# Four graph-attention layers over sixteen graphs: one-head weights by halves of the targets, a new timetable for the preparation of steps

## The chip, the cores and the metric

The kernel runs on one core of one Trainium2 chip. The metric is the device time of one execution in microseconds (us); the engines of the core are TensorE (PE, with its weight loads PEld), VectorE (DVE), ScalarE (ACT), GpSimd (POOL) and SyncE (SP, which here only issues transfers).

## The reference

x is 16 graphs x 1024 nodes x 256 features, adj one 1024 x 1024 matrix for all of them. Four layers follow each other; layers 0 and 2 have 4 heads of 64 features, layers 1 and 3 one head of 256:

```
h = relu(layernorm(x))
q = h @ W_l                                     # N x 256, as H heads of D
e[i, j] = leaky_relu(q_i . a_src + q_j . a_dst) # masked by adj[i, j]
x = x + act(softmax_j(e) @ q)                   # act: elu, in the last layer relu
```

All of it is float32. In the kernel exp(e[i, j]) is, up to factors of i alone, exp(slope * e_dst[j]) * max(G[i], R[j]), with G a row over the targets i and R a column over the sources j. So a block of softmax weights is one VectorE instruction, `max(G, R[j]) * mask`, and the sum of a softmax row is one more column of q.

## The kernel before

A **step** is one layer of one graph (64 steps, 32 with four heads and 32 with one). Four graphs are under way at a time, and `order_of_steps` lets them take turns; the order is mostly 4-head, 1-head, 4-head, 1-head, but in every eight steps two 4-head steps (13 and 14, 21 and 22, ..., 53 and 54) and two 1-head steps (17 and 18, ...) are neighbours. Steps 0, 1, 2 have four heads.

**Aggregation** of a step is cut into 8 groups (L323-326). A group of a 4-head step is one head and half of the targets: 64 matmuls (128 records in the profile, since a float32 matmul shows as two). A group of a 1-head step is 128 targets: 8 matmuls, 16 records. A group reads tiles `w` (L249): one tile holds the weights of 128 sources to all 1024 targets, a head has 8 of them, and a group of either kind needs all 8 sources' tiles. There are 19 buffers of `w`. The sums `acc` go to `y` on ACT (L270).

**Weights** (L250) are written by DVE, one tile an instruction, out of the head's row G. That row is made in the step's preparation: TensorE transposes it (L223), it goes to DRAM as `grow` (L227), comes back broadcast over the partitions as `gs` (L239, SP queue), and ACT copies it to PSUM as `g` (L245).

**Preparation** of a step (L149-234) is 18 pieces: statistics in two halves (DVE, L161-162, then four small POOL instructions, L165-169), normalisation (ACT, L175), transposes (PE, L183, then ACT, L184), eight projections (PE, L195, each followed by three ACT instructions, with four heads by one of POOL too), `factors` (ACT) and `rows` (L222-227).

**Finish** of a step (L274-318): the reciprocal on DVE (L287), the scaling on POOL, the exponential on ACT (L300), the maximum on DVE (L306), the sum into x on POOL (L307); after the last layer the store, and then the load of the next graph, on SP.

**Order.** Under `tc.manual_schedule()` (L387) every engine executes in the order in which the program emits. Time in the emission is counted in groups: 8 * step + group. The preparation of step n + 2 is planned at the start of step n, or at its group 4 if the graph's previous layer was step n - 1; `PREPARATION` gives the distance of each piece, `rows` at 9. As soon as `rows` of a step is emitted, its G may be fetched and copied, and DVE's tiles follow: 4 a group in a 4-head step, 2 in a 1-head step, as far as buffers allow. What follows a group in the emission: pieces of the finish of the step before, pieces of the preparation, tiles. The preparations of steps 0 and 1 stand ahead of the manual region, where the framework orders the instructions.

The lines that matter for the order:

```
            for k, (h, i0, per) in enumerate(groups(n)):
                if n + 2 < len(steps) and k == (0 if ready_at[n + 2] < n - 1 else 4):
                    plan(n + 2, 8 * n + k)
                emit_tiles(place[n, h, C - 1] + 1, must=True)
                aggregate(n, h, i0, per)
```

Of the kernel before, what the change touches and what calls it, by code (L numbers as in the profile page):

```python
# [24 lines left out]
F32 = mybir.dt.float32  # L25
# [4 lines left out]
ALU = mybir.AluOpType  # L30
# [3 lines left out]
P = 128  # L34
# [1 line left out]
SHIFT = 60.0  # L36
EXP_SHIFT = math.exp(SHIFT)
STREAMS = 4
WBUFS = 19
PREPARATION = (0, 0, 1, 2, 3, 3, 4, 4, 5, 5, 5, 5, 6, 6, 7, 7, 8, 9)  # L40


LAYERS = [
# [8 lines left out]
def kernel(ctx: ExitStack, tc: tile.TileContext, x, adj, ws, avs, out):  # L52
    nc = tc.nc
    B, N, F = x.shape
    C = N // P
    K = F // P
    HALF = C // 2
# [70 lines left out]
            for m, op in ((0, ALU.is_gt), (1, ALU.not_equal)):  # L128
                nc.vector.tensor_scalar(masks[m][:, :, ic * P:(ic + 1) * P], pm, 0.0, None, op0=op)

    xpool = ctx.enter_context(tc.tile_pool(name="xpool", bufs=STREAMS))
    prep = ctx.enter_context(tc.tile_pool(name="prep", bufs=2))
    small = ctx.enter_context(tc.tile_pool(name="small", bufs=4))
    work = ctx.enter_context(tc.tile_pool(name="work", bufs=2))
# [7 lines left out]
    xs = {}  # L142
    state = [dict() for _ in steps]

    def load(b):
        xs[b] = xpool.tile([P, C, F], F32, name="x")
        nc.sync.dma_start(out=xs[b], in_=x[b].rearrange("(c p) f -> p c f", p=P))

    def preparation(n):  # L149
# [19 lines left out]
                nc.gpsimd.tensor_scalar(shift, shift, -1.0, None, op0=ALU.mult)  # L169

        def normalise(half):
            xn = st["xn", half] = prep.tile([P, HALF, F], F32, name="t4", bufs=3)
            for q in range(HALF):
                c = half * HALF + q
                nc.scalar.activation(xn[:, q, :], xs[b][:, c, :], AF.Identity,  # L175
                                     bias=st["shift"][:, c:c + 1], scale=st["rstd"][:, c:c + 1])
# [54 lines left out]
            out += [lambda half=half, k=k: transpose(half, k) for k in range(K)]  # L231
            out += [lambda c=c: project(c) for c in range(half * HALF, (half + 1) * HALF)]

        return list(zip(PREPARATION, out + [factors, rows], strict=True))

    def fetch(n, h):

        gs = state[n]["gs", h] = work.tile([P, N], F32, name="gs", bufs=2)
        nc.sync.dma_start(out=gs, in_=state[n]["grow"][h].rearrange("c i -> (c i)")  # L239
                          .partition_broadcast(P))  # L240

# [2 lines left out]
        g = state[n]["g", h] = ps_g.tile([P, N], F32, name="g")  # L244
        nc.scalar.activation(g, state[n]["gs", h], AF.Copy)  # L245

    def weights(n, h, jc):

        w = state[n]["w", h, jc] = work.tile([P, N], F32, name="w", bufs=WBUFS)  # L249
        nc.vector.scalar_tensor_tensor(w, state[n]["g", h], state[n]["rcol"][:, jc, h:h + 1],  # L250
                                       masks[LAYERS[steps[n][1]][3]][:, jc, :],
                                       op0=ALU.max, op1=ALU.mult)

    def aggregate(n, h, i0, per):
        H = LAYERS[steps[n][1]][0]
        D = F // H
        st = state[n]
        if h == 0 and i0 == 0:
            st["y"] = work.tile([P, C, H, D + 1], F32, name="y")
        acc = ps_acc.tile([P, per, D + 1], F32, name="acc")  # L260
        cols = P // 2 if H > 1 else P
        for q in range(per):
            for jc in range(C):

                for o in range((i0 + q) * P, (i0 + q + 1) * P, cols):
                    nc.tensor.matmul(acc[o % P:o % P + cols, q, :],  # L266
                                     lhsT=st["w", h, jc][:, o:o + cols],
                                     rhs=st["whx"][:, jc, h, :], start=(jc == 0),
                                     stop=(jc == C - 1))
        nc.scalar.activation(st["y"][:, i0:i0 + per, h, :], acc, AF.Copy)  # L270

    def finish(n):

        b, l = steps[n]  # L274
        H = LAYERS[l][0]
        D = F // H
        st = state[n]

        def views(half):
            s = slice(half * HALF, (half + 1) * HALF)  # L280
            return (xs[b][:, s, :].rearrange("p c (h d) -> p (c h) d", h=H),
                    st["y"][:, s, :, 0:D].rearrange("p c h d -> p (c h) d"),
                    st["r"][:, s, :].rearrange("p c h -> p (c h)"))

        def divide():
            st["r"] = small.tile([P, C, H], F32, name="r")
            nc.vector.reciprocal(st["r"], st["y"][:, :, :, D])  # L287

        def scaled(half):
            xh, yh, r = views(half)  # L290
            nc.gpsimd.tensor_tensor(yh, yh, r[:, :, None].to_broadcast([P, HALF * H, D]),  # L291
                                    op=ALU.mult)
            if l < L - 1:

                e = st["e", half] = prep.tile([P, HALF * H, D], F32, name="t4", bufs=3)
                nc.gpsimd.tensor_scalar(e, yh, 0.0, -3.0e38, op0=ALU.min, op1=ALU.max)  # L296

        def exponential(half):
            if l < L - 1:
                nc.scalar.activation(st["e", half], st["e", half], AF.Exp)  # L300

        def add(half):
            xh, yh, r = views(half)
            if l < L - 1:
                e = st["e", half]
                nc.vector.scalar_tensor_tensor(e, e, -1.0, yh, op0=ALU.add, op1=ALU.max)  # L306
                nc.gpsimd.tensor_add(xh, xh, e)  # L307
                return
            nc.vector.scalar_tensor_tensor(xh, yh, 0.0, xh, op0=ALU.max, op1=ALU.add)
            nc.sync.dma_start(  # L310
                out=out[b, half * HALF * P:(half + 1) * HALF * P, :].rearrange(
                    "(c p) f -> p c f", p=P), in_=xs[b][:, half * HALF:(half + 1) * HALF, :])
            if half == 1 and b + STREAMS < B:
                load(b + STREAMS)

        return [(0, divide), (0, lambda: scaled(0)), (1, lambda: scaled(1)),
                (1, lambda: exponential(0)), (2, lambda: exponential(1)),
                (2, lambda: add(0)), (3, lambda: add(1))]

    def groups(n):  # L323
        if LAYERS[steps[n][1]][0] == 1:
            return [(0, i, 1) for i in range(C)]
        return [(h, i, HALF) for h in range(LAYERS[steps[n][1]][0]) for i in (0, HALF)]

    tiles = [(n, h, jc) for n, (b, l) in enumerate(steps) for h in range(LAYERS[l][0])
             for jc in range(C)]
    place = {t: i for i, t in enumerate(tiles)}  # L330
    done = {"tiles": 0, "g": 0, "gs": 0, "free": 0, "prepared": 0, "wanted": 0}
    agenda = []

    def prepare(upto):

        while agenda and (agenda[0][0] <= upto or agenda[0][1] < done["wanted"]):
            _, n, piece, last = agenda.pop(0)
            piece()
            if last:
                done["prepared"] = n + 1  # L340
                fetch_heads()

    def plan(n, at):
        new = preparation(n)
        agenda.extend((at + k, n, piece, i == len(new) - 1) for i, (k, piece) in enumerate(new))
        agenda.sort(key=lambda a: a[:2])

    def fetch_heads():

        while done["gs"] < min(done["g"] + 2 * C, len(tiles)):  # L350
            n, h, _ = tiles[done["gs"]]
            if n >= done["prepared"]:
                break
            fetch(n, h)
            done["gs"] += C

    def emit_tiles(upto, must=False):
        while done["tiles"] < min(upto, len(tiles)):
            i = done["tiles"]

            while done["g"] <= min(i + C // 2, len(tiles) - 1):
                n, h, _ = tiles[done["g"]]
                if n >= done["prepared"]:
                    if i < done["g"] or not must:
                        break
                    done["wanted"] = n + 1
                    prepare(-1)
                broadcast(n, h)
                done["g"] += C
                fetch_heads()  # L370
            if i >= done["g"]:
                return
            weights(*tiles[i])
            done["tiles"] += 1

    for b in range(STREAMS):
        load(b)
    ready_at = [-1] * len(steps)
    last = {}
    for n, (b, l) in enumerate(steps):  # L380
        ready_at[n] = last.get(b % STREAMS, -9)
        last[b % STREAMS] = n
    for n in range(2):
        plan(n, -99)
        prepare(0)
    ending = []
    with tc.manual_schedule():  # L387
        for n in range(len(steps)):
            for k, (h, i0, per) in enumerate(groups(n)):

                if n + 2 < len(steps) and k == (0 if ready_at[n + 2] < n - 1 else 4):
                    plan(n + 2, 8 * n + k)
                emit_tiles(place[n, h, C - 1] + 1, must=True)
                aggregate(n, h, i0, per)
                if i0 + per == C:
                    done["free"] = place[n, h, C - 1] + 1
                while ending and ending[0][0] <= k:
                    ending.pop(0)[1]()
                prepare(8 * n + k)
                ahead = 4 if per > 1 else 2  # L400
                emit_tiles(min(done["tiles"] + ahead, done["free"] + WBUFS))
            for _, piece in ending:
                piece()
            ending = finish(n)
        for _, piece in ending:
            piece()
# [38 lines left out]
```

## Time and profile before

| what | value |
|---|---|
| median of 3 runs (lowest to highest) | 2752.87 us (2752.55 to 2753.47) |
| the profiled execution: its time / its span | 2758.29 us / 2756.5 us |
| mean granted TensorE clock | 0.987 |
| PE busy | 2581.3 us, 94% |
| PEld busy | 2268.5 us, 82% |
| DVE busy | 1984.5 us, 72% |
| ACT busy | 1199.6 us, 44% |
| POOL busy | 896.6 us, 33% |
| `w`, 128 x 1024, L250 | 1280 instructions, mean 1273 ns |
| `g` <- `gs`, L245 | 160 instructions, mean 1022 ns |
| statistics, L161 and L162 | 512 each, mean 392 and 181 ns |

Two instructions in a row on an engine overlap a little, so a run of `w` moves on by 1.20 us a tile though one lasts 1.27 us. Lines are those of the kernel before; a timeline line gives start, duration (of a merged run), engine, line, what is written from what, its shape, how many, and in brackets the idle time before it with what ended it. "PEclk" is the share of the full TensorE clock that was granted.

### The profile page before, as it was taken

The page shows a single profiled execution, that of the slowest core. Times are in us where ns is not written, and L with a number is a line of the kernel's source. Part 1 is how long each engine was busy: PE and PEld are TensorE (multiplying, and loading weights), DVE is VectorE, ACT ScalarE, POOL GpSimd, SP SyncE. Part 2 cuts the span into 40 slices and gives each one's busy share as a digit, 9 for nine tenths or more (in the row PEclk, how much of TensorE's full clock was granted, in tenths as well). Part 3 has the DMA queues.
Part 4 walks back from the last instruction along what each step waited for, and adds up shares of the span by engine and source line. Part 5 has one row for each costly group of instructions (what it writes and reads, how often), then busy time and mean ns, then how long its engine had stood idle before and what let it go on. Part 6 is the DMA issues. An engine that isn't in the chain of part 4 may idle for free.

```text
span 2756.5 us, 88771 instructions
## 1 busy us (share of the span) xinstructions
PE 2581.3 (94%) x40080; PEld 2268.5 (82%) x40080; DVE 1984.5 (72%) x2569; ACT 1199.6 (44%) x3265; POOL 896.6 (33%) x909
## 2 busy tenths in 40 slices
PE   1789988999999999999999999999999999999997
PEld 1688777888888888888888888888888888888876
DVE  5596855767966779747977679767797488775772
ACT  0534444444444444544444445444444444444341
POOL 0223333343332343342242343333323333433221
PEclk9999999999999999999999999999999999999998
DMA  4111010012211210111211111002112111101101
GB/s 138 62 49 40 10 40 25 25 36 67 72 36 44 71 49 25 41 39 47 88 41 48 62 40 41 33 17 71 56 49 71 34 46 64 34 17 39 56 25 39
DMA packets 63674, 130.08 MB, mean 47 GB/s; under 512 B 6208, under 2 KB 41792, under 8 KB 63296
## 3 DMA queue, kind: packets, MB, share of 16 engines
q1 hardware_dynamic: 60608, 123.35, 13.4%
q8 instruction: 315, 5.16, 0.8%
q10 hardware_dynamic: 2688, 1.05, 0.2%
q14 instruction: 63, 0.52, 0.1%
HBM read 106.95 MB, written 17.43 MB: 45 GB/s over the span
## 4 chain that ended last, share of the span: by engine, by line
PE 72%; DVE 14%; DMA 6%; ACT 4%; issue 3%; POOL 1%; DVEq 0%; ACTq 0%; SPq 0%; POOLq 0%
PE acc L266 53%; PE pp L195 15%; DVE w L250 11%; DMA gs<-grow 4%; PE pp L183 3%; DMA grow<-gT 2%; DVE bn L161 1%; ACT t L300 1%; ACT g L245 1%; DVE t L306 1%; DVE mv L162 1%; ACT whx L197 1%; DMA a_bc<-in_L_gnn_a 1%; ACT whx L201 0%; ACT y L270 0%
## 5 line engine op out<-in xcount | busy, mean ns | idle before, releaser
L266 PE MATMUL acc<-whx,w 128*64 128x65 f32 x36864 | 1965.4, 242 | 77.9 <-DVE w L250 56.9
L266 PEld LDWEIGHTS acc<-whx,w 128*64 128x64 f32 x36864 | 1764.3, 145 | 265.5 <-DVE w L250 78.7
L250 DVE SCALAR_TENSOR_TENSOR w<-g,rcol,mask 128x1024 f32<-128x1024 f32 x1280 | 1543.3, 1273 | 523.4 <-ACT g L245 432.7
L270 ACT ACTIVATE y<-acc 128x260 f32<-128x260 f32 (+1 forms) x512 | 196.8, 384 | 1071.1 <-PE acc L266 1069.8
L195 PE MATMUL pp<-wx,hT 128*128 128x258 f32 (+1 forms) x2048 | 515.8, 395 | 2.9 <-ACT hT L184 2.7
L291 POOL TENSOR_TENSOR y<-y,r 128x1024 f32<-128x1024 f32 x128 | 243.0, 1899 | 716.1 <-DVE r L287 716.1
L195 PEld LDWEIGHTS pp<-wx,hT 128*128 128x128 f32 x2048 | 378.3, 192 | 78.1 <-ACT hT L184 15.7
L307 POOL TENSOR_TENSOR x<-x,t 128x1024 f32<-128x1024 f32 x96 | 226.8, 2362 | 408.2 <-DVE t L306 399.6
L206 POOL TENSOR_TENSOR whx<-whx 128x256 f32<-128x256 f32 x256 | 157.5, 618 | 471.2 <-ACT whx L204 471.2
L175 ACT ACTIVATE t<-x,shift,rstd 128x256 f32<-128x256 f32 x512 | 264.8, 588 | 78.7 <-POOL x L307 56.6
L245 ACT ACTIVATE g<-gs 128x1024 f32<-128x1024 f32 x160 | 163.5, 1022 | 129.5 <-DMA gs<-grow 128.0
L197 ACT ACTIVATE whx<-pp,nbias 128x4 f32<-128x4 f32 (+1 forms) x512 | 135.5, 265 | 181.3 <-PE pp L195 169.7
L161 DVE BATCH_NORM_STATS2 bn<-x 128x6 f32<-128x256 f32 x512 | 200.7, 392 | 2.4 <-DMA x<-in_x 2.4
L183 PE MATMUL pp<-ident,t 128*128 128x128 f32 x1024 | 155.4, 284 | 34.0 <-ACT t L175 18.9
L183 PEld LDWEIGHTS pp<-ident,t 128*128 128x128 f32 x1024 | 111.3, 141 | 78.8 <-ACT whx L201 28.0
L184 ACT ACTIVATE hT<-pp 128x512 f32<-128x512 f32 x256 | 145.5, 593 | 19.2 <-PE pp L183 18.8
L306 DVE SCALAR_TENSOR_TENSOR t<-t,y 128x1024 f32<-128x1024 f32 x96 | 118.4, 1233 | 35.4 <-ACT t L300 35.3
L287 DVE RECIPROCAL r<-y 128x32 f32<-128x32 f32 (+1 forms) x64 | 17.6, 276 | 160.0 <-ACT y L270 159.9
L201 ACT ACTIVATE whx<-pp,whx 128x256 f32<-128x256 f32 x256 | 121.7, 475 | 0.0
L166 POOL TENSOR_TENSOR rstd<-rstd,neghalf 128x8 f32<-128x8 f32 x64 | 106.7, 1668 | 5.3
L162 DVE BATCH_NORM_AGGREGATE mv<-bn 128x2 f32<-128x6 f32 x512 | 92.8, 181 | 16.9
L296 POOL TENSOR_SCALAR t<-y 128x1024 f32<-128x1024 f32 x96 | 101.7, 1060 | 8.5
(37 smaller groups left out, 533.0 us busy)
## 6 DMA issues: line engine op xcount, KB each, us to landing
gs<-grow SPq DMA_DIRECT2D x160, 512.0 KB
x<-in_x SPq DMA_DIRECT2D x16, 1024.0 KB
out<-x SPq DMA_DIRECT2D x32, 512.0 KB
a_raw<-in_adj SPq DMA_DIRECT2D x8, 512.0 KB
a_bc<-in_L_gnn_a ACTq DMA_DIRECT2D x8, 128.0 KB
wx<-in_L_gnn_W SPq DMA_DIRECT2D x4, 256.0 KB
grow<-gT SPq DMA_DIRECT2D x32, 16.0 KB
grow<-gT SPq DMA_DIRECT2D x32, 4.0 KB
```

What stands on the lines that cost most here:

```text
L161: nc.vector.bn_stats(st["bn"][:, c, :], xs[b][:, c, :])
L175: nc.scalar.activation(xn[:, q, :], xs[b][:, c, :], AF.Identity, bias=st["shift"][:, c:c + 1], scale=st["rstd"][:, c:c + 1])
L183: nc.tensor.transpose(pt[:, q, :], st["xn", half][:, q, k * P:(k + 1) * P], ident)
L195: nc.tensor.matmul(pw, lhsT=st["hT", half][:, k, q * P:(q + 1) * P], rhs=wx[l][:, k, :], start=(k == 0), stop=(k == K - 1))
L197: nc.scalar.activation(whx[:, c, :, D], pw[:, F + H:F + 2 * H], AF.Exp, bias=nbias[l], scale=slope)
L206: nc.gpsimd.tensor_tensor(whx[:, c, :, 0:D], whx[:, c, :, 0:D], whx[:, c, :, D:D + 1].to_broadcast([P, H, D]), op=ALU.mult)
L245: nc.scalar.activation(g, state[n]["gs", h], AF.Copy)
L250: nc.vector.scalar_tensor_tensor(w, state[n]["g", h], state[n]["rcol"][:, jc, h:h + 1], masks[LAYERS[steps[n][1]][3]][:, jc, :], op0=ALU.m ...
L266: nc.tensor.matmul(acc[o % P:o % P + cols, q, :], lhsT=st["w", h, jc][:, o:o + cols], rhs=st["whx"][:, jc, h, :], start=(jc == 0), stop=(j ...
L270: nc.scalar.activation(st["y"][:, i0:i0 + per, h, :], acc, AF.Copy)
L291: nc.gpsimd.tensor_tensor(yh, yh, r[:, :, None].to_broadcast([P, HALF * H, D]), op=ALU.mult)
L307: nc.gpsimd.tensor_add(xh, xh, e)
```

## The change

- `WBUFS` goes from 19 to 17, the x buffers from 4 to 5, the `gs` buffers from 2 to 1 (one row is fetched ahead, not two). The shared tile `t4` becomes `xn` and `e` with two buffers each.
- A tile of a 1-head step holds two sources for half of the targets, in two DVE instructions of 512 columns. The first four groups of the step need the first four tiles only, and these are free after group 3.
- A preparation starts at `begin[n]`: 8 * (n - 2) for a 1-head step, 4 less for a 4-head step, not before group 4 of the step after the graph's last one, nor before 4 groups after the preparation before. Its pieces have new distances, of which there are two lists; two pieces are added, which fetch the row and declare the step prepared (copies of G are emitted from then on): `rows` at 10 and prepared at 12 for one head, 11 and 13 for four.
- The stores are pieces of their own (groups 4 and 5), with the next load behind them. The fifth x is loaded at step 1.
- The preparations of steps 0 and 1 now stand inside the manual region.

```diff
-WBUFS = 19
-PREPARATION = (0, 0, 1, 2, 3, 3, 4, 4, 5, 5, 5, 5, 6, 6, 7, 7, 8, 9)
+WBUFS = 17
+PREPARATION = {
+    1: (0, (0, 0, 2, 3, 4, 4, 5, 5, 6, 6, 6, 6, 7, 7, 8, 8, 9, 10, 10, 12)),
+    4: (-4, (0, 0, 2, 3, 4, 4, 7, 7, 7, 7, 7, 7, 9, 9, 9, 9, 10, 11, 11, 13)),
+}
...
-        return list(zip(PREPARATION, out + [factors, rows], strict=True))
+        return [(begin[n] + k, piece) for k, piece in
+                zip(PREPARATION[H][1], out + [factors, rows, lambda: fetch_heads(n + 1), lambda: None],
+                    strict=True)]
...
+        if H > 1:
+            parts = [(t, 0, N)]
+        else:
+            parts = [(t % HALF * 2 + i, t // HALF * (N // 2), N // 2) for i in range(2)]
+        for i, (jc, o, size) in enumerate(parts):
+            st["w", h, jc, o] = w[:, i * size:(i + 1) * size]
+            nc.vector.scalar_tensor_tensor(
+                st["w", h, jc, o], st["g", h][:, o:o + size], st["rcol"][:, jc, h:h + 1],
+                masks[mask][:, jc, o:o + size], op0=ALU.max, op1=ALU.mult)
...
-        while done["gs"] < min(done["g"] + 2 * C, len(tiles)):
+        done["rows"] = max(done["rows"], below)
+        while done["gs"] < min(done["g"] + C, len(tiles)):
             n, h, _ = tiles[done["gs"]]
-            if n >= done["prepared"]:
+            if n >= done["rows"]:
                 break
...
                 if n >= done["prepared"]:
                     if i < done["g"] or not must:
                         break
-                    done["wanted"] = n + 1
-                    prepare(-1)
+                    prepare(max(a[0] for a in agenda if a[1] == n))
...
+        begin.append(8 * (n - 2) + PREPARATION[LAYERS[l][0]][0] if n > 1 else -99)
+        if b in last:
+            begin[n] = max(begin[n], 8 * (last[b] + 1) + 4)
+        if n > 2:
+            begin[n] = max(begin[n], begin[n - 1] + 4)
...
-    for n in range(2):
-        plan(n, -99)
-        prepare(0)
     with tc.manual_schedule():
+        for planned in (1, 2):
+            plan(planned - 1)
+            prepare(-1)
         for n in range(len(steps)):
+            if n == 1:
+                load(by_last[STREAMS])
             for k, (h, i0, per) in enumerate(groups(n)):
-                if n + 2 < len(steps) and k == (0 if ready_at[n + 2] < n - 1 else 4):
-                    plan(n + 2, 8 * n + k)
-                emit_tiles(place[n, h, C - 1] + 1, must=True)
+                plan_up_to(8 * n + k)
+                half = LAYERS[steps[n][1]][0] == 1
+                emit_tiles(place[n, h, HALF - 1 if half and i0 < HALF else C - 1] + 1, must=True)
                 aggregate(n, h, i0, per)
-                if i0 + per == C:
-                    done["free"] = place[n, h, C - 1] + 1
+                if i0 + per == C or (half and i0 + per == HALF):
+                    done["free"] = place[n, h, C - 1 if i0 + per == C else HALF - 1] + 1
```

## The prediction

> **What bounds the kernel now.** I read the page's busy table first (PE 94%), then PE by stretches of time, since a mean hides stages. In the middle a 4-head group takes 3.91 us (two: 7.83) and a 1-head group 3.54, and PE hardly waits. It waits at the two ends. The stretches (PE busy, PEld, DVE, ACT, POOL, granted clock, DMA share, GB/s):
>
> ```profile
> 330.00:385.00 55.00, 51.98 (x242) 40.55 (x240) 23.04 (x33) 26.92 (x83) 19.29 (x19) 0.94 0.10 30
> 385.00:435.00 50.00, 38.58 (x1023) 35.94 (x1024) 49.50 (x64) 14.08 (x27) 15.13 (x13) 0.93 0.08 24
> 435.00:480.00 45.00, 44.41 (x229) 37.21 (x227) 12.04 (x16) 24.20 (x76) 17.34 (x18) 1.00 0.10 36
> 480.00:530.00 50.00, 42.70 (x1033) 38.78 (x1031) 45.17 (x53) 19.66 (x47) 13.19 (x11) 0.93 0.08 24
> 530.00:610.00 80.00, 78.89 (x430) 66.80 (x426) 42.75 (x71) 38.54 (x109) 33.06 (x31) 1.00 0.10 34
> ```
>
> Steps 6 (384 to 433) and 8 (479 to 532) are bound by DVE, which was idle just before: their rows of G came late. In the middle PE waits in two ways. First, DVE at pairs of 4-head steps; DVE in the first step of the pair that starts at S = 1011.84, and PE in the second:
>
> ```profile
> 1024.42 1.21 DVE L306 SCALAR_TENSOR_TENSOR t<-t,y 128x1024 f32<-128x1024 f32 x1
> 1025.55 4.85 DVE L250 SCALAR_TENSOR_TENSOR w<-g,rcol,mask 128x1024 f32<-128x1024 f32 x4
> 1030.32 1.21 DVE L306 SCALAR_TENSOR_TENSOR t<-t,y 128x1024 f32<-128x1024 f32 x1
> 1031.45 23.92 DVE L250 SCALAR_TENSOR_TENSOR w<-g,rcol,mask 128x1024 f32<-128x1024 f32 x20
> ```
> ```profile
> 1061.08 0.92 PE L266 MATMUL acc<-whx,w 128*64 128x65 f32 x24
> 1062.24 0.34 PE L266 MATMUL acc<-whx,w 128*64 128x65 f32 x4 [0.24 <-DVE w L250]
> 1063.43 6.87 PE L266 MATMUL acc<-whx,w 128*64 128x65 f32 x228 [0.85 <-DVE w L250]
> ```
>
> A first row of 4 matmuls takes 0.12 us, so 1.19 between starts is 1.07 lost; this pair loses 3.5 us in all. Second, ACT stands at a copy of G whose row is still in flight, and the next `acc` is not evacuated. From the waits (total, times, longest):
>
> ```profile
> ACT g L245 <- DMA gs<-grow: 128.0, 34, 5.8
> ...
> PEld acc L266 <- ACT y L270: 25.7, 24, 2.0
> ...
> PE acc L266 <- ACT y L270: 18.1, 19, 1.6
> ```
>
> So 128 us on ACT cost PE 18 to 26.
>
> **The change part by part** (own time 2758.29, 5.4 above the runs' median 2752.87; I apply the sum to the median). The order of instructions of both programs gave the places.
>
> *Copies two groups behind their rows.* From the PE transpose of G (370.11 in step 5) to the first tile (378.10) it takes 8.0 us; two groups are 7.1 to 7.8 plus projections, so ACT no longer waits: **-20** (bounds 0 and -30).
>
> *Statistics.* Counting statistics by step in both orders: 32 of 62 stand in 4-head steps before, 37 after (the preparations of steps 0 and 1 left out), and thirteen of these steps hold two, at groups 0 and 4 (8, and 13, 16, 21, 24 and so on), because the neighbouring 4-head steps shift the rhythm. One takes DVE 4.25 us (1010.7 to 1014.9). In step 21 after: 14 tiles are ready when the step starts at S (17 buffers, the last freed in group 7); reciprocal at S+0.6 (`y` and it follow PE's end by 0.5, as at 1010.6); statistics to S+5.0; tiles 15 to 29 and two maxima, 15 x 1.20 + 2 x 1.13 = 20.2, to S+25.2; second statistics to S+29.45; tiles 30 to 32 to S+33.0. PE: six groups 23.4, transposes 1.0, two projections 1.95; it wants tile 32 0.85 us into the group, at S+27.3. Stall 5.8 for 3.5 before. Steps 16, 24, ... likewise, but two projections ahead of S let DVE start 1.9 us earlier and PE comes 2.1 later: 1.8 for 0. Six of each: 14 + 11 = **+25**. Bounds: all such stalls gone, -21; six with a slow clock behind them, +48: a run of 120 1-head matmuls at 2715.51, after a wait, took 29.84 for 120 x 0.216 = 25.9, in a stretch with a clock of 0.87, so up to 3.9 each.
>
> *Steps 6 and 8.* `rows` of a 4-head step stands at distance 11, not 9. The bound is begin = 36 for step 6 (its graph ended in step 3), as before. So `rows` moves from group 5 to group 7 of step 5; what remains of its preparation and that of step 7 is forced out before group 0 of step 6. Before, PE's transpose at 370.11 was 13.9 us ahead of the step, after it is four projections, 3.5 us. From that transpose to the end of the step DVE sets 61.9 us (to 431.98: 32 tiles, statistics, two maxima, PE's last two groups), unchanged. +10; step 8 the same: **+20** (10 to 24).
>
> *Start.* The preparations of steps 0 and 1 were interleaved by the framework (the second's POOL statistics at 70.8); now they stand in sequence on each engine, the second's behind the first's `gcol` (88.2). From there: POOL 2.6, normalise 4.0, relu 1.1, four projections 3.6, transposes and relu 2.1, four 3.6, evacuation, factors, `gT` 2.7, copy 1: first tile near 109 for 97.59. Steps 0 to 2 hang on DVE (first tile to last, 97.6 to 239.0: 133 of 141 us busy), so most arrives; four projections of step 4 move behind step 2: **+12** (4 to 16). Steps 3 to 5: late rows there too, but two waits (1.8 and 4 us) go: **+1** (-4 to +5).
>
> *End.* The last step's preparation: statistics wait for group 4 of step 62, so transposes, eight projections, factors, row, copy are all forced between steps 62 and 63: relu after normalise 3.7, four projections 3.6, transposes and relu 2.4, four 3.6, evacuation and factors 2, 8.0 to the first tile, that is 23.3; then 1.8 because the first group waits for 8 half tiles (5.3 for 3.5) and 2.5 for a slow clock; less 9.4 of PE work, which is done anyway: 18, for 6.5 before (PE late from 2709 to 2719). Step 60 loses a late row and late transposes, -6. **+5** (0 to 14).
>
> *PE's order.* Transposes right behind projections wait for `pp` (0.2 + 0.2, and 0.15 at the switch): 67 such places become 85, +9; interruptions of 4-head groups fall from 185 to 155 at 0.2, -6: **+3** (-3 to +9).
>
> *Half tiles.* 256 more DVE instructions. Between the row of 256 elements (392 ns) and of 1024 (1273) a 512 takes about 690, two 1380: 0.1 us more a tile, 27 us of DVE; bounds 0 (half of 1273) and 38. They lie under the 1-head groups, where DVE idles (22 us ahead of step 6); without that cover a 1-head step would pay 0.9. **0** (-2 to +5). Five x buffers and the stores: SP has groups to spare, **0**.
>
> [...]
>
> Sum: -20 + 25 + 20 + 12 + 1 + 5 + 3 = **+46**: 2752.87 + 46 = 2799, I say **2800 us** (on the own time 2804).
>
> The clock: it was 0.93 in the two DVE-bound stretches, 1.00 between them; of the six pairs two (740 to 790, 2030 to 2080) show 0.97. [...]
>
> **Rivals.**
> - *Early rows free DVE* (faster). The place is group 6 of the 4-head steps, the point that decides is tile 32 ready by S+27.3: if rows that arrive early let DVE be that far, the pairs lose nothing (-21 for +25), and ACT's waits give their upper bound (-30 for -20). With the rest as summed (+41): -10, **2743**. For: 128 us of waits on ACT and 433 us in which DVE waited for `g` in the page's waits. Against: it needs DVE 5.8 us earlier, so 19 tiles ready at S, and there are 17 buffers. Chance 0.09.
> - *A draw.* The pairs' stalls vanish, the copies give 20: 0, **2753**. 0.06.
> - *Worse.* The statistics don't leave the 4-head steps, so the change doesn't do what it says, and the stalls slow the clock: +48 for +25, start 16, end 14: **2835**. 0.13.
> - *As summed*, 2770 to 2825: 0.72.
>
> The range 2765 to 2840 leaves out the faster case, the draw, and a little above: under 0.2. A measurement of this kernel tells 0.2% (5.5 us) from no change. Faster 0.09, same 0.06, slower 0.85.
>
> **What would show it.** First tile near 108; steps 6 and 8 near 58 to 62 us; PE idle for DVE of some 6 us once in step 21, none in 22; 23 us idle ahead of step 63; ACT's wait for `gs` under 20 us outside the forced places. Wrong if DVE is ready at group 6 of steps 21 and 24, or the first tile still comes before 100.

## The result, and the profile after

The changed kernel takes 2842.8 us (median of 4 runs, 2841.1 to 2846.6) for 2752.7 (4 runs, 2750.6 to 2753.5): ratio 1.033, 95% interval 1.031 to 1.035. The direction was forecast, the size was not: 90 us were lost, not 46, and 2842.8 lies above the range's end of 2840. The profiled execution took 2842.5 us, its span is 2840.7 for 2756.5, and its mean clock 0.967 for 0.987.

To see where, I give each step an **excess**: over its PE instructions, the time from one start to the next, less the usual spacing of that shape (0.0303 us for 65 columns, 0.216 for 257, 0.217 to 0.222 for a projection, 0.109 for a transpose). The starts of the steps then split the 84.2 us between the two spans (a step starts with its first matmul of `acc`, so a wait for its first tile counts in the step before):

| stretch | before | after | difference |
|---|---|---|---|
| to the start of step 3 | 252.8 | 272.4 | +19.6 |
| steps 3 to 5 | 131.2 | 143.9 | +12.7 |
| steps 6 to 8 | 148.4 | 162.1 | +13.7 |
| steps 9 to 59 | 2057.0 | 2094.5 | +37.5 |
| step 60 to the end of the span | 167.1 | 167.8 | +0.7 |

The stretches of steps 4, 6 and 8 after (PE busy, PEld, DVE, ACT, POOL, granted clock, DMA share, GB/s):

```profile
306.00:363.00 57.00, 48.06 (x1082) 43.54 (x1081) 44.03 (x65) 24.51 (x60) 15.57 (x15) 0.91 0.09 30
...
416.00:470.00 54.00, 42.38 (x1026) 39.43 (x1027) 53.27 (x66) 10.67 (x19) 12.93 (x10) 0.76 0.12 41
...
522.00:578.00 56.00, 46.79 (x1064) 42.25 (x1065) 54.24 (x68) 20.33 (x45) 13.28 (x11) 0.83 0.12 39
```

DVE fills 53 to 54 us of steps 6 and 8, PE waits for it, and step 4, which lost 3.1 us before, is 57 us long. The waits of the whole run (total, times, longest):

```profile
DVE w L265 <- PE acc L282: 141.9, 38, 6.8
PEld acc L282 <- DVE w L265: 139.5, 143, 7.4
...
PE acc L282 <- DVE w L265: 116.6, 118, 7.2
...
ACT g L252 <- DMA gs<-grow: 20.5, 7, 5.0
```

ACT's wait for rows of G has gone from 128.0 to 20.5, as forecast. What grew is DVE's wait for a free `w` buffer and with it PE's wait for `w`; before, these were:

```profile
DVE w L250 <- PE acc L266: 57.7, 21, 3.0
PE acc L266 <- DVE w L250: 56.9, 84, 1.2
```

Step 24 shows both, on DVE and on PE; it starts at S = 1189.37, and the statistics at its groups 0 and 4 end at 1192.5 and 1219.2:

```profile
1192.47 3.63 DVE L265 SCALAR_TENSOR_TENSOR w<-g,rcol,mask 128x1024 f32<-128x1024 f32 x3
1198.38 4.86 DVE L265 SCALAR_TENSOR_TENSOR w<-g,rcol,mask 128x1024 f32<-128x1024 f32 x4 [2.27 <-PE acc L282]
...
1219.19 14.17 DVE L265 SCALAR_TENSOR_TENSOR w<-g,rcol,mask 128x1024 f32<-128x1024 f32 x19
```
```profile
1217.91 0.80 PE L282 MATMUL acc<-whx,w 128*64 128x65 f32 x20
1220.50 0.34 PE L282 MATMUL acc<-whx,w 128*64 128x65 f32 x4 [1.78 <-DVE w L265]
1221.69 0.34 PE L282 MATMUL acc<-whx,w 128*64 128x65 f32 x4 [0.86 <-DVE w L265]
1222.88 4.71 PE L282 MATMUL acc<-whx,w 128*64 128x65 f32 x100 [0.85 <-DVE w L265]
```

DVE had time at the start of the step and could not use it: with 17 buffers tile 18 waits until PE has done head 0, 9.0 us into the step. Later it has no time, and PE waits at group 6 for the last three tiles.

Mean excess in steps 9 to 59 (us a step; medians in us; "issued" counts in the order of instructions how many tiles of a 4-head step DVE has been given when PE's first matmul of that step comes). The experiments' rows are read below:

| kernel | median | issued | 13, 21, ... | 14, 22, ... | 16, 24, ... | 11, 19, ... | 1-head | step 9 starts |
|---|---|---|---|---|---|---|---|---|
| before | 2752.7 | 13 | 1.7 | 5.2 | 1.7 | 1.4 | 1.9 | 532.4 |
| after | 2842.8 | 14, 13 | 8.4 | 1.6 | 7.6 | 1.6 | 1.1 | 578.4 |
| e1_stats | 2835.5 | 14, 13 | 7.3 | 1.6 | 7.2 | 1.6 | 1.1 | 580.3 |
| e4_bufs | 2823.5 | 14 | 8.3 | 1.6 | 4.2 | 1.8 | 1.1 | 580.4 |
| e8_late | 2796.3 | 14, 13 | 3.3 | 2.9 | 2.5 | 1.6 | 1.4 | 578.5 |
| e15_full | 2876.6 | 11 | 10.8 | 1.8 | 8.1 | 2.0 | 1.1 | 585.1 |
| e10_acopy | 3021.4 | 15, 13 | 8.1 | 1.6 | 8.1 | 1.8 | 7.7 | 595.6 |
| e5_b17 | 2856.5 | 11 | 6.7 | 7.5 | 6.6 | 5.9 | 1.8 | 534.3 |
| e6_bcopies | 2881.9 | 10 | 7.6 | 7.3 | 7.6 | 7.2 | 0.9 | 558.1 |
| e11_lead | 2751.4 | 15 | 1.9 | 4.5 | 1.6 | 1.2 | 0.9 | 555.5 |
| e7_bhalf | 2734.4 | 14 | 1.6 | 3.8 | 1.4 | 1.3 | 1.8 | 528.9 |
| e12_best | 2715.8 | 19, 15 | 1.6 | 3.5 | 1.5 | 1.3 | 0.9 | 531.2 |

### The profile page after: what moved, and what is told of

The parts are those of the page before. It is cut to its first block, busy times and chain, and to the rows that moved or that the text cites. A ratio compares the mean times of both kernels' runs of the same rounds, so it can differ in the third digit from the quotient of the medians.

```text
span 2840.7 us, 89053 instructions
## 1 busy us (share of the span) xinstructions
PE 2615.5 (92%) x40080; PEld 2298.9 (81%) x40080; DVE 2023.3 (71%) x2825; ACT 1215.6 (43%) x3265; POOL 902.9 (32%) x909
## 4 chain that ended last, share of the span: by engine, by line
PE 73%; DVE 18%; ACT 4%; issue 3%; DMA 2%; POOL 1%; DVEq 0%; POOLq 0%; ACTq 0%; SPq 0%
PE acc L282 55%; PE pp L199 15%; DVE w L265 13%; PE pp L187 3%; DVE bn L165 2%; DVE mv L166 1%; ACT whx L205 1%; ACT whx L201 1%; DVE e L322 1%; DVE x L325 1%; DMA gs<-grow 1%; ACT xn L179 1%; DMA a_bc<-in_L_gnn_a 1%; ACT g L252 0%; ACT whx L208 0%
## 5 line engine op out<-in xcount | busy, mean ns | idle before, releaser
L282 PE MATMUL acc<-whx,w 128*64 128x65 f32 x36864 | 1987.6, 246 | 119.2 <-DVE w L265 116.6
L282 PEld LDWEIGHTS acc<-whx,w 128*64 128x64 f32 x36864 | 1801.2, 149 | 291.2 <-DVE w L265 139.5
L265 DVE SCALAR_TENSOR_TENSOR w<-g,rcol,mask 128x1024 f32<-128x1024 f32 (+1 forms) x1536 | 1576.7, 1094 | 540.6 <-ACT g L252 398.6
L323 POOL TENSOR_TENSOR x<-x,e 128x1024 f32<-128x1024 f32 x96 | 227.3, 2368 | 246.4 <-DVE e L322 238.3
L179 ACT ACTIVATE xn<-x,shift,rstd 128x256 f32<-128x256 f32 x512 | 263.9, 588 | 10.2 <-POOL shift L173 10.2
L322 DVE SCALAR_TENSOR_TENSOR e<-e,y 128x1024 f32<-128x1024 f32 x96 | 121.6, 1266 | 124.3 <-ACT e L316 124.3
L187 PE MATMUL pp<-ident,xn 128*128 128x128 f32 x1024 | 161.2, 286 | 39.0 <-ACT xn L179 19.7
L187 PEld LDWEIGHTS pp<-ident,xn 128*128 128x128 f32 x1024 | 111.8, 142 | 93.6 <-ACT whx L205 44.6
L252 ACT ACTIVATE g<-gs 128x1024 f32<-128x1024 f32 x160 | 162.9, 1018 | 41.4 <-DVE w L265 20.9
L169 POOL TENSOR_SCALAR rstd<-mv 128x8 f32<-128x8 f32 x64 | 15.5, 242 | 384.1 <-DVE mv L166 384.0
L222 POOL TENSOR_SCALAR gcol<-gcol 128x32 f32<-128x32 f32 (+1 forms) x64 | 22.1, 345 | 338.5 <-ACT gcol L220 338.4
## 6 DMA issues: line engine op xcount, KB each, us to landing
a_bc<-in_L_gnn_a ACTq DMA_DIRECT2D x8, 128.0 KB
```

The lines of the kernel that those rows point to most:

```text
L187: nc.tensor.transpose(pt[:, q, :], st["xn", half][:, q, k * P:(k + 1) * P], ident)
L265: nc.vector.scalar_tensor_tensor(st["w", h, jc, o], st["g", h][:, o:o + size], st["rcol"][:, jc, h:h + 1], masks[mask][:, jc, o:o + size], ...
L282: nc.tensor.matmul(acc[o % P:o % P + cols, q, :], lhsT=st["w", h, jc, origin][:, o - origin:o - origin + cols], rhs=st["whx"][:, jc, h, :] ...
```

## The experiments

The kernel before, beside the experiments, took 2752.1 to 2754.7 us, so a difference of 2 or 3 us between two runs of this section means nothing.

**e1_stats: no 4-head step behind step 8 holds two statistics.**

```diff
+        m = begin[n] // 8
+        early = 4 if (n > 8 and H == 1 and begin[n] % 8 == 0 and LAYERS[steps[m][1]][0] > 1
+                      and LAYERS[steps[m - 1][1]][0] == 1) else 0
-        return [(begin[n] + k, piece) for k, piece in
+        return [(begin[n] + k - (early if i < 2 else 0), piece) for i, (k, piece) in enumerate(
...
-        while planned < len(steps) and begin[planned] <= now:
+        while planned < len(steps) and begin[planned] - 4 <= now:
```

> The changed kernel, with one preparation's statistics four groups earlier wherever they would be the second in a 4-head step: they then stand in the 1-head step before it, and no 4-head step holds two. Theory (two statistics in one 4-head step are the largest loss): the twelve steps 13, 16, 21, 24 and so on, whose PE time beyond its own matmuls is 7.2 to 9.8 us each, fall to the 1.6 us of the steps that hold one already (11, 19, 27): 12 x 5.8 = 70 us off, about 2773. Rival (17 buffers of w set how far DVE is ahead, and the statistics only show it): DVE gets back 4.25 us of the 5.6 to 8 that each step loses and the rest stays as waits for a free buffer, 1.4 to 3 us in each: about 2795. Should neither be so (the stalls come from PE's own order), it stays within 10 us of 2843.

2835.5 us, 7 off: neither the theory nor its rival, only the last number of the three, and PE's own order, the reason given with that number, is not what the trace shows: PE still waits for `w`. The 7 us lie in steps 13, 37 and 53, which lose some 2.4 us less each. Step 24, on DVE and on PE:

```profile
1197.97 4.86 DVE L268 SCALAR_TENSOR_TENSOR w<-g,rcol,mask 128x1024 f32<-128x1024 f32 x4 [5.89 <-PE acc L285]
```
```profile
1220.11 0.34 PE L285 MATMUL acc<-whx,w 128*64 128x65 f32 x4 [1.79 <-DVE w L268]
1221.30 0.34 PE L285 MATMUL acc<-whx,w 128*64 128x65 f32 x4 [0.85 <-DVE w L268]
1222.49 4.55 PE L285 MATMUL acc<-whx,w 128*64 128x65 f32 x100 [0.86 <-DVE w L268]
```

Of the 4.25 us that DVE saved at group 0, 3.6 went into its wait for a buffer (5.89 for 2.27) and 0.5 into one for `g`, and PE's stalls are the same to 0.01 us. So statistics at group 0 are free here, and my theory of "two in one step" falls.

**e2_start and e3_early: the start, in two parts.** First the initial preparations outside the hand-ordered region; then the old distances for steps 2 to 8.

```diff
-    with tc.manual_schedule():
-        for planned in (1, 2):
-            plan(planned - 1)
-            prepare(-1)
+    for planned in (1, 2):
+        plan(planned - 1)
+        prepare(-1)
+    with tc.manual_schedule():
```

> The changed kernel, with the preparations of steps 0 and 1 outside the region in which the order is fixed by hand, as in the kernel before; nothing else differs. Theory: the first tile comes at 98 us instead of 111, and as DVE sets the pace up to step 3 the 12 to 15 us are kept: about 2830. Rival: steps 4, 6 and 8 start late through their own rows, whatever came earlier, and take the gain back: 2838 or more.

2826.4 us, 16.4 off: as the theory said. PE's first group starts at 103.0 for 112.4, and step 9 16.2 us earlier.

```diff
+EARLY = (0, 0, 1, 2, 3, 3, 4, 4, 5, 5, 5, 5, 6, 6, 7, 7, 8, 9, 9, 9)
...
+        times = PREPARATION[H][1] if n > 8 else EARLY
-                zip(PREPARATION[H][1], out + ...
+                zip(times, out + ...
```

> The changed kernel, with the distances of the kernel before (rows of G at 9 and the copy with them) for the preparations of steps 2 to 8 alone; all later steps keep the new ones. Theory (late rows at the start of steps 4, 6 and 8): step 4 loses the 13 us that it gained and steps 6 to 8 the 15 us: about 2816, step 4 near 43 us, step 6 near 49, step 8 near 53. Rival (17 buffers and the statistics hold DVE in these steps): step 4 stays above 50 us, and the time above 2832.

2816.2 us, 26.6 off, as the theory said: step 4 takes 44.2 us (57.0), step 6 49.3 (53.4), step 7 45.0 (52.3). Step 8 keeps 55.2, but PE's wait of 4.9 us for its first tile, which counts in step 7, is gone. So the later distances, of the rows and of the copies behind them, are the cause there; no buffers were changed.

**e4_bufs: 19 buffers again.**

```diff
-WBUFS = 17
+WBUFS = 19
...
-    masks = [const.tile([P, C, N], U8, name=f"mask{i}") for i in range(2)]
+    masks = [const.tile([P, C, N], U8, name="mask")] * 2
```

> The changed kernel with 19 buffers for w as before. The space comes from keeping one mask for both kinds of layer: the same instructions write and read it, but the second kind of layer is computed with the wrong mask. Theory (buffers and statistics together): DVE enters each 4-head step two tiles (2.4 us) further ahead, so the twelve stalled steps lose 2.4 us less each and steps 4, 6 and 8 something: 2843 - 29 - 4 = 2810. Rival (statistics alone): DVE is late by its work and not by its buffers, 2837 to 2846. Second rival (buffers alone): the stalls go whole, under 2790.

2823.5 us, 19.3 off, midway between the first theory (2810) and its rival (2837 or more). (adj holds 0 and 1 alone, so one mask serves both kinds of layer, other than the expectation says.) Steps 16, 24, ... lose 3.4 us less each, the pairs next to nothing: buffers are a part, not the whole. Step 21 of the changed kernel (S = 1065.28) shows why: from tile 15 on, behind the statistics at group 0, DVE writes seven tiles there without a wait, so a further buffer has nothing to give.

```profile
1070.02 8.40 DVE L265 SCALAR_TENSOR_TENSOR w<-g,rcol,mask 128x1024 f32<-128x1024 f32 x7
```

**e8_late: the statistics of group 4 at group 0 of the next step.** (Normalisation and first transposes of that preparation move too, by three and two groups. In the changed kernel they are emitted behind the matmuls of group 6, so the stall there is not theirs.)

```diff
+        times = PREPARATION[H][1]
+        if H == 4 and n > 8 and LAYERS[steps[begin[n] // 8][1]][0] == 4:
+            times = (4, 4, 5, 6, 6, 6) + times[6:]
...
```

> The changed kernel; where the preparation of a 4-head step begins at group 4 of a 4-head step, its statistics, normalise and first transposes come 4, 3 and 2 groups later, so the statistics stand at group 0 of the next step. Taking the other statistics, those at group 0, out of the 4-head steps left step 24 at 7.4 us beyond its matmuls (7.5 with them): DVE only waited 5.89 instead of 2.27 us for a free buffer of w. New theory: at group 0 statistics are free, since DVE waits there for PE to free head 0's buffers; after that release DVE has 15 tiles, two maxima and, at group 4, statistics of 4.25 us, and those make tile 32 late. The twelve steps fall to 1.6 to 3 us: 12 x 5 = 60 off, about 2783. Rival (the 17 buffers alone set it): steps 21 and 24 stay above 6 us, 2830 or more. Second rival (PE's own other work, 3 us instead of 10 ahead of group 6 in these steps, is what lets PE come early): half goes, about 2810.

2796.3 us, 46.5 off. That is midway between the theory (2783) and its second rival (2810); the steps speak for the theory: steps 13, 21, ... and 16, 24, ... are within 1.6 us of their loss in the kernel before (3.3 and 2.5 in the table), where the rival has half of it stay. Steps 13, 16, 21, 24 and so on hold one statistics here as in e1_stats, at group 0 for group 4; that is worth 39 us, from 2835.5 to 2796.3 (the second steps of the pairs hold one more here, steps 11, 19, ... one less). Step 24, on DVE and on PE:

```profile
1186.78 4.86 DVE L268 SCALAR_TENSOR_TENSOR w<-g,rcol,mask 128x1024 f32<-128x1024 f32 x4 [2.27 <-PE acc L285]
...
1198.59 18.96 DVE L268 SCALAR_TENSOR_TENSOR w<-g,rcol,mask 128x1024 f32<-128x1024 f32 x23
```
```profile
1206.31 3.95 PE L285 MATMUL acc<-whx,w 128*64 128x65 f32 x128
```

The wait for a buffer is as long as in the changed kernel, but behind it nothing stands between the tiles and the maxima, and PE runs through group 6. The 46.5 are less than the 60 expected: some 3 us stay in the first steps of the pairs, and the second ones lose 1.3 more. Steps 11, 19, ... hold theirs at group 4 in the changed kernel and lose nothing: in the order of instructions PE has ten projections ahead of group 6 there, four in step 24. That this gives DVE its time is argued, not tried.

**e9_all: e2, e3 and e8 together.**

> Three edits at once on the changed kernel: initial preparations outside the hand-ordered region (alone 16 us off), the old distances up to step 8 (alone 27 off), the statistics of group 4 four groups later. If the new theory of the statistics holds and the parts add: 2843 - 16 - 27 - 60 = 2740, faster than the kernel before by its copies behind their rows. If the statistics are not it: 2790 to 2800. If the parts overlap (steps 4 to 8 hold both): up to 2750.

2747.2 us, ratio to the kernel before 0.9973 (0.996 to 0.9987). The three parts nearly add (16.4 + 26.6 + 46.5 = 89.5; 95.6 measured) and together take the whole loss back.

**e5_b17: the kernel before with `WBUFS = 17`.**

> The kernel before with 17 instead of 19 buffers for w and nothing else. Theory (two buffers are two tiles of lead, 2.4 us of DVE, in steps where tile 32 is just in time): stalls of about 2 us in the six pairs and some in the other 4-head steps, 10 to 25 us in all, about 2770. Rival (only with statistics at group 4 do buffers matter): within 5 us of 2753.

2856.5 us, 102 lost: four times the theory's upper end, and the rival is out. Step 24 on PE (starts at 1165.9):

```profile
1184.58 0.34 PE L266 MATMUL acc<-whx,w 128*64 128x65 f32 x4 [0.73 <-DVE w L250]
1186.90 4.71 PE L266 MATMUL acc<-whx,w 128*64 128x65 f32 x100 [1.99 <-DVE w L250]
```

The kernel before stood at an edge: with 13 tiles issued at the start of a 4-head step only six steps stall, with 11 all of them do, some 5 us each.

**e6_bcopies and e11_lead: the late copies alone.** The kernel before with copies from distance 11; then also four tiles after each group.

```diff
-PREPARATION = (0, 0, 1, 2, 3, 3, 4, 4, 5, 5, 5, 5, 6, 6, 7, 7, 8, 9)
+PREPARATION = (0, 0, 1, 2, 3, 3, 4, 4, 5, 5, 5, 5, 6, 6, 7, 7, 8, 9, 9, 11)
...
+        done["rows"] = max(done["rows"], below)
-            if n >= done["prepared"]:
+            if n >= done["rows"]:
                 break
...
```
```diff
-                ahead = 4 if per > 1 else 2
+                ahead = 4
```

> The kernel before with one part of the change: the copy of G of the next step comes two groups after its row (fetch at distance 9, copy from 11), all else as it was. Theory (ACT's waits for rows held up evacuations): 20 us off, 2733, and ACT's wait for gs from 128 us to under 30. Rival (the copy that comes later delays the first tiles of a step and DVE has less lead): 2753 or more, with more stalls at the starts of steps 4, 6 and 8.

> The kernel before with the copies two groups behind their rows (2882 alone), and four tiles of w, not two, issued after each group of a 1-head step. Counted in the order of instructions, DVE has 13 tiles of a 4-head step issued when PE starts it in the kernel before, 11 with 17 buffers (2856), 10 with the late copies (2882), 15 here. Theory (this lead is the quantity: the late copies lost through three tiles of it, not through the copies themselves): the 127 us come back and the 20 us of ACT's waits as well, 2715 to 2740, 4-head steps near 41 us. Rival (the copy itself is late, however many tiles are issued): 2840 or more. Second rival (the lead helps, but nothing is gained from ACT): 2750 to 2760.

2881.9 us, 127 lost, in the rival's direction and far more than its "2753 or more" suggests: in the old timetable the copy of the next row comes in group 3 of a 1-head step, two tiles follow each group, and only 10 tiles are issued when the 4-head step starts. ACT's waits are gone, and all 4-head steps lose 7 us. With four tiles a group 15 are issued and 130 us come back: the lead was what the late copies had cost. The number, 2751.4 (0.9987 to 1.0006 of before), is the second rival's, not the theory's, but it hides two parts: steps 9 to 59 are 31 us shorter than before (2025.9 for 2057.0), most of it in the 1-head steps (0.9 for 1.9 us each), where that rival has nothing gained; and step 9 starts 23 us later, as it does in e6_bcopies (26), so late copies cost in the first steps, where rows are late anyway.

**e7_bhalf and e15_full: the half tiles, alone in the kernel before, and taken out of the changed one.**

```diff
-        if H > 1:
+        if True:
             parts = [(t, 0, N)]
...
-        origin = 0 if H > 1 else i0 // HALF * (N // 2)
+        origin = 0
-                half = LAYERS[steps[n][1]][0] == 1
+                half = False
```

(That is e15_full; e7_bhalf adds the same lines of the change to the kernel before.)

> The kernel before with the weights of 1-head steps by halves of the targets, and nothing else. Theory (33 us more on DVE, under 1-head groups in which DVE idles; half a step's buffers come free earlier): within 6 us of 2754. Rival (DVE's lead at the start of the 4-head steps shrinks by the slower 1-head tiles): 10 to 33 us slower. Second rival (buffers that come free at the middle of a 1-head step give DVE more lead): 10 to 25 us faster.

> The changed kernel with whole tiles of w in the 1-head steps again; 17 buffers and all else as changed. DVE then has 11 tiles of a 4-head step issued when PE starts it, for 14 in the changed kernel. Theory (lead at the start of the 4-head steps is what the half tiles are worth, since half a step's buffers come free in its middle): 24 steps lose 3 to 5 us each, 2915 to 2960. Rival (as predicted: the half tiles cost and bring nothing): 2837 to 2849.

e7_bhalf 2734.4 us, ratio 0.9938 (0.9923 to 0.9952): 18 faster. e15_full 2876.6: 34 slower than the changed kernel, less than the theory's 70 to 120 and far from nothing. Buffers that come free in the middle of a 1-head step let DVE have one tile more issued in the kernel before (14 for 13), three more in the changed one (14 for 11).

**e10_acopy and e14_gs2: the changed kernel with copies beside their rows, with one row buffer and with two.**

```diff
-    1: (0, (0, 0, 2, 3, 4, 4, 5, 5, 6, 6, 6, 6, 7, 7, 8, 8, 9, 10, 10, 12)),
-    4: (-4, (0, 0, 2, 3, 4, 4, 7, 7, 7, 7, 7, 7, 9, 9, 9, 9, 10, 11, 11, 13)),
+    1: (0, (0, 0, 2, 3, 4, 4, 5, 5, 6, 6, 6, 6, 7, 7, 8, 8, 9, 10, 10, 10)),
+    4: (-4, (0, 0, 2, 3, 4, 4, 7, 7, 7, 7, 7, 7, 9, 9, 9, 9, 10, 11, 11, 11)),
```
```diff
-        gs = state[n]["gs", h] = work.tile([P, N], F32, name="gs", bufs=1)
+        gs = state[n]["gs", h] = work.tile([P, N], F32, name="gs", bufs=2)
-        while done["gs"] < min(done["g"] + C, len(tiles)):
+        while done["gs"] < min(done["g"] + 2 * C, len(tiles)):
```

(e14_gs2 has both, and shares `t4` as before for the space.)

> The changed kernel with the copy of G in the group of its row again, two groups earlier; fetch, statistics and all else as in the changed kernel. Theory (the copies behind their rows are worth 20 us): about 2863, ACT's wait for gs above 100 us again, 1-head steps 1.2 us longer. Rival (earlier copies give DVE more lead, which weighs more): 2830 or less. Second rival (both cancel): 2837 to 2849.

> The changed kernel with the copies beside their rows (3021 with one buffer for the row gs), and with two buffers for gs, fetched two heads ahead as before; the buffer's space comes from xn and e sharing three buffers again. Theory (with one gs buffer ACT waits for a row, copies, and waits for the next; that made 178 us of a cost of some 20): 2855 to 2885. Rival (the early copy itself, in the changed timetable, blocks ACT ahead of normalise and the evacuations): above 2950.

3021.4 and 3036.3 us: 179 and 193 lost. None of e10_acopy's three numbers comes near, the second buffer takes nothing back, and e14_gs2's rival holds. e10_acopy around the start of step 23 (1213.7), on ACT, DVE and PE:

```profile
1219.95 1.03 ACT L252 ACTIVATE g<-gs 128x1024 f32<-128x1024 f32 x1 [5.72 <-DMA gs<-grow]
```
```profile
1221.01 4.86 DVE L265 SCALAR_TENSOR_TENSOR w<-g,rcol,mask 128x1024 f32<-128x1024 f32 x4 [9.41 <-ACT g L252]
1225.79 0.35 DVE L303 RECIPROCAL r<-y 128x32 f32<-128x32 f32 x1
```
```profile
1238.74 0.33 PE L187 MATMUL pp<-ident,xn 128*128 128x128 f32 x1 [4.33 <-ACT xn L179]
```

The row is emitted in group 7, so the copy that waits for it, and four tiles that wait for the copy, now stand ahead of the last step's reciprocal on DVE. All that follows it (scaling, exponential, then normalise behind it on ACT) comes late, and PE waits for `xn`. ACT stands at that copy for 5.72 us with the next evacuation of `acc` behind it, as the rival has it; the way over DVE's reciprocal stands in neither expectation.

**e13_last: the last statistics behind the addition.** In the kernel before the statistics and the normalisation of step 63 read graph 15's x ahead of layer 2's addition to it, so its last layer works on an x without that addition; the changed kernel waits for it.

```diff
-                    plan(n + 2, 8 * n + k)
+                    plan(n + 2, 8 * n + k + (8 if ready_at[n + 2] == n else 0))
```

> The kernel before with one thing changed: the statistics of the last preparation (step 63, the same graph as step 61) come at group 4 of step 62, behind the addition of layer 2 to x, as in the changed kernel; before, they stand at group 4 of step 61 and read x ahead of that addition. Theory (the end of the changed kernel is longer by this dependency, not by its timetable): 5 to 15 us more, 2758 to 2768. Rival: the last row is late in any case and nothing changes, 2750 to 2756.

2765.3 us, ratio 1.0041 (1.0029 to 1.0053): 13 us, as the theory said. The excess of step 62 goes from 8.1 to 19.0, and the first tile of step 63 waits 28.97 us for its `g`, for 18.11 before:

```profile
2716.71 9.62 DVE L250 SCALAR_TENSOR_TENSOR w<-g,rcol,mask 128x1024 f32<-128x1024 f32 x8 [28.97 <-ACT g L245]
```

**e12_best: the kernel before with what paid** (half tiles, late copies and four tiles a group from step 9 on, and e13's order at the end).

```diff
-                ahead = 4 if per > 1 else 2
+                ahead = 4 if per > 1 or n > 8 else 2
-        return list(zip(PREPARATION, out + ...
+        return list(zip(PREPARATION[:-1] + (11 if n > 8 else 9,), out + ...
```

> The kernel before with the parts that paid alone: half tiles (18 off), copies two groups behind their rows from step 9 on with four tiles issued after each group of a 1-head step (31 off in steps 9 to 62 when the loss at the start is left out). DVE's lead at the 4-head steps is 19 tiles, or 15 in the second step of a pair. Its last preparation waits until layer 2 of the same graph has been added to x, which the kernel before does not (about 8 us longer). If the parts add: 2753 - 18 - 31 + 8 = 2712. If lead beyond 13 is worth nothing and the halves only gave lead: 2730. If the order issues 1-head tiles too early and they stand before the maxima: 2745 or more.

2715.8 us, ratio 0.9855 (0.9837 to 0.9873): the parts add, and it beats both kernels. Its waits:

```profile
PEld acc L275 <- DVE w L258: 67.9, 99, 7.2
PE acc L275 <- DVE w L258: 45.6, 48, 7.0
ACT g L245 <- DMA gs<-grow: 21.0, 6, 5.9
DVE w L258 <- PE acc L275: 5.6, 6, 1.6
```

DVE waits 5.6 us for buffers, not 57.7 as before or 141.9 as in the changed kernel.

## Why the prediction was right in sign and wrong in size

- **Statistics, +25: the step that failed, measured +55** (excess of the 4-head steps from 11 to 59: 61.7 before, 116.8 after). In the pairs the working held: 5.4 us more in steps 21, 29 and 45 (forecast 5.8), 3.6 less in the second steps (forecast 3.5). It failed for steps 16, 24 and so on: "two projections ahead of S let DVE start 1.9 us earlier ...: 1.8 for 0" became 5.9 each. DVE did start early, and lost it in the wait for head 0's buffers (2.27 us in step 24), which the working had left out and which two projections behind group 0 make longer. The count of two statistics was the wrong quantity: e1_stats shows the one at group 0 to be free, e8_late the one at group 4 to cost, and two more buffers are worth 3.4 us in each of these steps (e4_bufs).
- **The clock.** Steps 13, 37 and 53 lose 2.5 us more than 21, 29 and 45. Their stalls are followed by two slow windows, those of step 21 by one, and the mean clock is 0.93 there (735 to 783, 1721 to 1769, 2380 to 2428) for 0.96 in steps 21 and 45 (1065 to 1110, 2052 to 2097); step 21 after, in windows of 4 us (clock third from the right):

```profile
1080.00:1084.00 4.00, 2.29 (x68) 2.01 (x64) 4.00 (x4) 3.22 (x7) 2.00 (x1) 0.97 0.00 0
1084.00:1088.00 4.00, 4.00 (x84) 3.93 (x81) 4.00 (x5) 0.25 (x2) 2.37 (x1) 0.60 0.40 135
1088.00:1092.00 4.00, 4.00 (x116) 3.83 (x116) 3.90 (x9) 1.41 (x3) 0.00 (x0) 1.00 0.02 4
...
1096.00:1100.00 4.00, 2.29 (x72) 2.13 (x72) 4.00 (x4) 1.03 (x1) 1.00 (x3) 1.00 0.02 4
```

  PE was idle 1.7 of 4 us, then at 0.60 for 4 us: the 100 matmuls behind the stall took 4.71 us, 1.6 more than the 3.14 of those at 1098.07. In step 13 it is 0.54 and 0.61 in two windows, and the same 100 took 5.67, 2.5 more. I kept this for the rival "Worse" and out of the sum. The same idle share 16 us later (the last row) was followed by 4 us at 1.00. So in step 21 two gaps of some 0.85 us came ahead of a slow window once, and once they did not; what decides it is not shown.
- **Start, +12 and +1: measured 19.6 to step 3 and 12.7 in steps 3 to 5.** The first tile came at 111.08, 13.5 later than before (forecast 109, 11.4 later). DVE's three waits for `g` behind it, 8.7 us in all, were 6.7 before, and PE now waits 2.4 us for the first tile of step 3, which it did not before. "Late rows there too, but two waits go" missed step 4: 8 tiles are issued at its start for 13 before. Of the 12.7, 4.9 belong to step 6 (next point). e2_start takes 12.5 of the 19.6 back, e3_early all of the 12.7.
- **Steps 6 and 8, +20: 17.4, and the cause was right.** PE waits for their first tiles, which it did not before:

```profile
416.30 0.49 PE L282 MATMUL acc<-whx,w 128*64 128x65 f32 x4 [4.93 <-DVE w L265]
...
522.07 0.49 PE L282 MATMUL acc<-whx,w 128*64 128x65 f32 x4 [4.93 <-DVE w L265]
```

  With these waits the steps take 58.3 and 61.2 us, as forecast, which is 9.4 and 8.0 more than before. The table's 13.7 for steps 6 to 8 has the first wait in steps 3 to 5.
- **Copies, -20: -19.4** in the changed kernel's 1-head steps 9 to 58 (excess 48.7 to 29.3). e6_bcopies, where the copies alone came later, has the same there (0.9 for 1.9 us a step). The term is right only for this pairing: alone in the old timetable the late copies cost 127, and putting them back beside their rows in the new one costs 179.
- **Half tiles, 0: the cost was, the gain was not.** They added 33 us of DVE (1543.3 to 1576.7, neighbours overlapping), 27 forecast, off the path. But they give lead: 18 us in the kernel before, 34 in the changed one. A 512 took 739 ns, not 690, and a 1024 took 1272.
- **17 buffers** had no term of their own; alone they cost over 100 us (e5_b17). In the changed kernel two more are worth 19 (e4_bufs) and the half tiles 34 (e15_full). That the halves make up for most of the two missing buffers fits this, but 17 buffers with halves in the old timetable were not tried. The change traded the one for the other, and I priced neither.
- **End, +5: +0.7.** From the last matmul of step 62 to the first of step 63 it is 23.3 us, as forecast, and step 60 gives 6.4 back (6 forecast). But step 62 loses only 8.4 us more, and step 63 with the end behind it is 4.1 shorter, 4.3 together where the sum had 11.5; step 61 loses 3.0 more. Which part of that working was too high is not shown; its 2.5 for a slow clock was an estimate without a working, and after the 23.3 us the clock was 0.50 (2796 to 2804) and the 128 matmuls from 2799.11 took 30.53 us, for 27.6 at the usual spacing. e13_last has the price of the late order alone, 13 us in the kernel before. **PE's order, +3**, was not tried by itself. Its waits lie within the excess of the 4-head (+55.1) and 1-head steps (-19.4), which leave 1.8 of the 37.5 in steps 9 to 59.

Of the rivals, "Worse" (2835) came nearest, by its size: slow windows did follow stalls (0.60 in step 21, 0.54 and 0.61 in step 13), and the mean clock went from 0.987 to 0.967. "Early rows free DVE" named a quantity that counts, tiles ready at S, but more of them than the buffers hold never come, and it is not the only one: the changed kernel has 14 issued, e10_acopy 15, and their stalls are longer than with 13 before, since the statistics at group 4 come on top. Not tried: the five x buffers and the stores by themselves.

## What to carry to other kernels

Where one engine fills buffers for another in bursts, count at the start of each burst how much has been issued ahead, and walk the burst from the moment when buffers come free: work that falls into the wait for a buffer is free, the same work behind it is paid in full. Price a smaller pool of buffers as an edit of its own, and ask of each edit what it does to that lead. Parts that cost or gain alone can do the opposite together, so one that is undone in the new kernel does not tell what it did in the old.

## What the runs showed of the hardware

In step 21 of the changed kernel two short waits of PE, 0.85 us each and within 3 us, were followed by 4 us at a granted clock of 0.60; two like them in the same step, 15 us later, by 4 us at 1.00. The durations on DVE and ACT were those of the trace of before (`w` of 1024 columns 1272 ns for 1273, the copy of G 1018 for 1022, statistics 395 and 182 for 392 and 181), and a `w` of 512 columns, new here, took 739; the surprise lay in the order of the instructions.
